# A four-layer graph network on one core: layer 2's early products in batches of six tiles, the totals' maximum ten steps later and pinned, count matrices spread to step 340

## The chip, the cores and the metric

The kernel runs on one core of a Trainium2 chip. A core has five engines that run side by side, each taking its own instructions in order: PE (TensorE, matrix products), DVE (VectorE), ACT (ScalarE), POOL (GpSimd) and SP (SyncE, which here only starts transfers). They meet through semaphores. PE reads SBUF and writes PSUM; DVE and ACT read both. Transfers between HBM and SBUF are started by SP, ACT or POOL. POOL starts the indirect ones (gathers), in which a list in SBUF names a row of a table in HBM for each of 128 partitions.

The metric is device time in microseconds (us). The profile is of one execution. Its matmuls are pipelined and their ends are modelled, so a PE that is busy throughout need not be at its peak.

## The reference

There are N = 6250 nodes with 256 features and E = 100000 edges, sorted by their target `dst`; `src` is random. The targets are dense at small node numbers: up to node n lie about E * sqrt(n / N) edges. The reference applies a layer norm and a relu, and then four graph layers and a last product:

```
deg = segment_sum(1, dst)
h = sage_mean(h):  h @ W1_self + (segment_sum(h[src], dst) / max(deg, 1)) @ W1_neigh + b1
h = sage_pool(h):  hp = relu(h @ W2_pool + b2_pool)
                   h @ W2_self + segment_max(hp[src], dst) @ W2_neigh + b2
h = sage_gcn(h):   ((segment_sum(h[src], dst) + h) / (deg + 1)) @ W3_neigh + b3
h = sage_mean(h):  the form of layer 1, with W4 and b4
return x + h @ W_fc + b_fc
```

Layer 2 is the one that counts here. It takes, for each node, the maximum over the rows `hp[src]` of its incoming edges, and from it and the node's own row the product that layer 3 sums up. The weights of the later layers are multiplied together beforehand, so that layer 2 hands on rows of 512 numbers.

## The kernel before

Nodes are handled in 49 tiles of 128. A row that is summed later is stored split into three bf16 parts (high, middle, low).

**Sums over edges** (layers 1, 3 and 4) are done in two ways. For the first 16 or 18 tiles, whose nodes have many edges, a count matrix says how often each source node occurs for each target node of the tile; the sum is then a dense product of count blocks (fp8, kept in the table `tab_a`) with the split rows. For the other tiles the rows are gathered edge by edge and added with one-hot matrices on PE.

**Layer 2's maximum.** The 100000 edges are laid out in 782 columns of 128 edges, in six blocks of 52, 100, 220, 180, 130 and 100 columns, which are handled from the last block (the largest node numbers) to the first. Each column is one step of the main loop, counted by `at`. In a step POOL gathers 128 rows of `hp` into a buffer X (L1339; a buffer holds two columns and there are six of them), and DVE combines them with the running maximum `run` (L1320, three operations in two steps). SP stores the running maxima that may be needed into `rows2` (L1324). At the end of a block, `carry` passes maxima across the 128 lanes: transposes on PE (L1185, L1208), scans on DVE, a gather (L1200), a maximum (L1211) and a store.

**Beside each step**, the loop issues other work, paced by `at`:

- Count matrices of tiles 8 to 17 (`build_narrow`). Each of 32 columns of a tile takes two one-hots: on DVE a mask `hm` (L363), on ACT `ht` and `hs` (L361, L368). PE multiplies them (L379), ACT copies the counts to the matrix A (L384), and SP stores A to `tab_a` (L388). The 256 columns of tiles 8 to 15 (`first`) are spread evenly from step 16 to step `EARLY_AT` (L1370), the 64 of tiles 16 and 17 (`rest`) from there to step 682 (L1372). One-hots run up to 12 columns ahead.
- `done2(d)`, for each node tile d from 48 down to 0, once the block in which its edges begin is done, and at least 11 steps apart. It is a generator that advances once per step. It gathers the tile's totals from `rows2`, one gather for each block that the tile's edges touch (one or two), and the tile's own rows `th` from `tab_t`. Six steps later it takes the maximum of two totals where there are two (L1235, DVE), and then, a step each: PE transposes (L1239), ACT copies the result to `hTf` (L1242), PE multiplies the own rows with `usA` and `usB` (L1246, L1249) and the maximum with `un` (L1252, two steps), and the sum is split into three bf16 parts `r3` by ACT casts with PE subtractions between (L1260 to L1268). SP stores `r3` to `tab_r`, layer 3's table (L1269).
- Early products of layer 3. As soon as `BATCH` tiles between 6 and 37 have their `r3`, `early_products` queues, for each of the 16 dense tiles of layer 3, a load of the count blocks `ae` (L1296, SP), three matmuls per batch tile (L553) and an addition to the sum `acc3` of that dense tile (L1110, DVE; the first time a copy on ACT, L1113). The loop issues one thirty-second of what is left in each step, at least one piece.

After the last step, the loop at L1400 finishes the tiles still open; tile 0 can begin only there, when the last block is done. Layer 3 gathers from `tab_r`, so its first gather (L472) waits until the last row of the table has landed.

**What sets the order.** The text above is the program's order. The compiler lays out each engine's instructions anew: it takes, by its own estimate of times, the earliest in program order among those that are ready, so work can run before or after its step. `tc.keep_in_program_order(ins)` ties an instruction behind the one that stands before it in the program on the same engine. All buffers of a name come from a ring of `bufs` copies, and an instruction that needs a new one waits until the oldest is free.

Of the kernel before, what the change touches and what calls it, by code (L numbers as in the profile page):

```python
# [9 lines left out]
F32 = mybir.dt.float32  # L10
# [5 lines left out]
ALU = mybir.AluOpType  # L16
# [4 lines left out]
P = 128  # L21
# [10 lines left out]
EARLY = (6, 38)  # L32
MADE_AT = 64
FIRST_AT = 112
EARLY_AT = 250


def _edges_below(n, E, N):
# [40 lines left out]
def fast_path(  # L79
# [15 lines left out]
    nc = tc.nc  # L95
# [10 lines left out]
    KI = FI // P  # L106
    KH = FH // P
# [97 lines left out]
    ident = const.tile([P, P], F32, name="identf")  # L205
# [41 lines left out]
    def bank(pool, tag, name, shape=None, bufs=None):  # L247
        t = pool.tile([P, FH], F32, tag=one_tag.get(id(pool), tag), name=name, **({"bufs": bufs} if bufs else {}))
        if shape is None:
            return t  # L250
        n = math.prod(shape)
        if len(shape) == 1:
            return t[:, :n]
        return t[:, :n].rearrange("p (a b) -> p a b", b=shape[1])
# [387 lines left out]
    with ExitStack() as pro:  # L642
        pst = pro.enter_context(tc.tile_pool(name="pst0", bufs=3, space=PSUM))
        psm = pro.enter_context(tc.tile_pool(name="psm0", bufs=3, space=PSUM))
# [97 lines left out]
        for c in range(NC):  # L742
            nc.tensor.matmul(pc[:, c : c + 1], under[:, c * P : (c + 1) * P], ones_b,
                             start=True, stop=True)
# [208 lines left out]
    with ExitStack() as on:  # L953
        pst = on.enter_context(tc.tile_pool(name="pst1", bufs=1, space=PSUM))
        psm = on.enter_context(tc.tile_pool(name="psm1", bufs=1, space=PSUM))
        psg = on.enter_context(tc.tile_pool(name="psg1", bufs=2, space=PSUM))
        psd = on.enter_context(tc.tile_pool(name="psd1", bufs=2, space=PSUM))
        wk = on.enter_context(tc.tile_pool(name="fl1", bufs=2))
# [4 lines left out]
        def done1(d, acc):  # L963
# [31 lines left out]
            for k in range(KI):  # L995
# [11 lines left out]
                        lambda acc, d=d: todo.append(done1(d, acc)), extra=3)  # L1007
# [107 lines left out]
    with tc.tile_pool(name="fl2c", bufs=1) as ck, ExitStack() as late:  # L1115
# [5 lines left out]
        usA = ck.tile([P, KI, FH], F32, name="usA")  # L1121
        usB = ck.tile([P, KI, FH], F32, name="usB")
# [55 lines left out]
        wk = late.enter_context(tc.tile_pool(name="fl2", bufs=2))  # L1178
# [37 lines left out]
        def totals(d):  # L1216
            tots = []
            for b in range(b_of[d][0], b_of[d][1] + 1):
                t = wk.tile([P, FH], F32, name="tot", bufs=4)
                nc.gpsimd.indirect_dma_start(  # L1220
                    out=t, out_offset=None, in_=rows2[0 : run_at[b] + n_of[b], :],
                    in_offset=bass.IndirectOffsetOnAxis(ap=rows_of[b][:, d : d + 1], axis=0),
                )
                tots.append(t)
            th = wk.tile([P, 2 * KI, P], F32, name="th2", bufs=4)
            nc.scalar.dma_start(th, tab_t[d].rearrange("p (k n) -> p k n", n=P))
            return tots, th

        def done2(d):
            tots, th = totals(d)  # L1230
            for _ in range(6):
                yield
            hm = tots[0]
            for t in tots[1:]:
                nc.vector.tensor_tensor(hm, hm, t, op=ALU.max)  # L1235
            yield
            pt = bank(pst, "pt", "pt_hTf", (KH, P))
            for j in range(KH):
                nc.tensor.transpose(pt[:, j, :], hm[:, j * P : (j + 1) * P], ident)  # L1239
            yield  # L1240
            hT = wk.tile([P, KH, P], F32, name="hTf")
            nc.scalar.copy(hT, pt)  # L1242
            yield
            pm = bank(psm, "pm", "pm_prf")
            for k in range(KI):
                nc.tensor.matmul(pm, th[:, k, :], usA[:, k, :], start=(k == 0), stop=False)  # L1246
            yield
            for k in range(KI):
                nc.tensor.matmul(pm, th[:, KI + k, :], usB[:, k, :], start=False, stop=False)  # L1249
            yield  # L1250
            for c in range(KH):
                nc.tensor.matmul(pm, hT[:, c, :], un[:, c, :], start=False, stop=(c == KH - 1))  # L1252
                if c == 1:
                    yield
            yield
            yield
            yield
            r3 = early_pool[0].tile([P, 3 * FH], BF16, name="r3", bufs=2 * BATCH + 1)
            hi, mid, lo = (r3[:, i * FH : (i + 1) * FH] for i in range(3))
            nc.scalar.copy(hi, pm)  # L1260
            yield
            nc.tensor.matmul(pm, minus_b, hi, start=False, stop=True, skip_group_check=True)
            yield
            nc.scalar.copy(mid, pm)
            yield
            nc.tensor.matmul(pm, minus_b, mid, start=False, stop=True, skip_group_check=True)
            yield
            nc.scalar.copy(lo, pm)  # L1268
            nc.sync.dma_start(tab_r[d * P : (d + 1) * P, :], r3)  # L1269
            if EARLY[0] <= d < EARLY[1]:  # L1270
                ready.append((d, r3))
                if len(ready) == BATCH or d == EARLY[0]:
                    early_products()
            yield


        BATCH = 4
        ready = []
        early = Hub()
        early_pool = []  # L1280
# [6 lines left out]
        def early_products():  # L1287
# [3 lines left out]
            for d in range(H3):  # L1291
                got = {}

                def load(d=d, got=got):
                    got[0] = early_pool[0].tile([P, BATCH, P], F8, name="ae", bufs=LOOK + 3)
                    nc.sync.dma_start(got[0][:, : len(ss), :].bitcast(BF16),  # L1296
                                      tab_a[d, :, ss[0] : ss[-1] + 1, :])
# [29 lines left out]
        tiles, begun2, begun_at = [], 0, 0  # L1327
        ends = []
        now = []
        at = 0  # L1330
        for b in reversed(range(NB)):
# [3 lines left out]
            for s0 in range(0, tb, G2):  # L1335
                X = (xmore if at // G2 % 2 else xpool).tile([P, G2, FH], F32, name="X2")
                for k in range(G2):
                    t = t0 + s0 + k
# [24 lines left out]
                    if at == MADE_AT:  # L1363
                        for _ in steps:
# [3 lines left out]
                            top.enter_context(tc.tile_pool(name="early3", bufs=1)))  # L1368
                    if at <= EARLY_AT:
                        hub.advance(math.ceil(len(first) * max(0, at - 16) / (EARLY_AT - 16)))  # L1370
                    else:
                        hub.advance(len(first) + math.ceil(  # L1372
                            len(rest) * (at - EARLY_AT) / (T - 100 - EARLY_AT)))
                    early.advance(early.done + math.ceil(early.left() / 32))
# [3 lines left out]
                    if (tiles and not ends and at >= begun_at + 11  # L1378
                            and begun2 < NT * (at - FIRST_AT) / (T - 20 - FIRST_AT)):
                        begun_at = at  # L1380
                        now.append(done2(tiles.pop(0)))
                        begun2 += 1
# [9 lines left out]
        tiles += [d for d in reversed(range(NT)) if b_of[d][0] == 0]  # L1392
        while tiles or now:
            if tiles and len(now) < 2:
                now.append(done2(tiles.pop(0)))
            for g in list(now):
                if next(g, 0) == 0:
                    now.remove(g)
# [42 lines left out]
    with ExitStack() as on:  # L1441
        psd = on.enter_context(tc.tile_pool(name="psd3", bufs=2, space=PSUM))
        psg = on.enter_context(tc.tile_pool(name="psg3", bufs=3, space=PSUM))
        psm = on.enter_context(tc.tile_pool(name="psm3", bufs=2, space=PSUM))
# [8 lines left out]
        with tc.tile_pool(name="fl3", bufs=2) as wk:  # L1453
# [36 lines left out]
            for d in range(H3):  # L1490
                work += dense([s for s0, s1 in late for s in range(s0, s1)], lambda s, d=d: block(d, s), lambda s: Z3[s], FH, psd,
                              lambda acc, d=d: todo.append(done3(d, acc)), own=d)
# [3 lines left out]
        with tc.tile_pool(name="fl4", bufs=2) as wk:  # L1496
# [22 lines left out]
            for d in range(H4):  # L1519
                parts4.append(dense([s for s0, s1 in order for s in range(s0, s1)],  # L1520
                                    lambda s, d=d: block(d, s), lambda s: Z4[s], FO, psd,
                                    lambda acc, d=d: todo.append(done4(d, acc)), wide=True))
# [652 lines left out]
```

## Time and profile before

| | |
|---|---|
| median of 3 runs | 2820.56 us (2816.73 to 2822.64) |
| the profiled execution's own time | 2817.91 us |
| its span, first to last instruction | 2816.1 us |
| mean granted PE clock | 0.932 |
| busy over the span: PE, DVE, ACT, POOL | 85%, 74%, 33%, 69% |
| layer 2's gathers L1339, first to last | 784.6 to 1905.4 us |
| layer 3's first gather L472 | 1943.5 us |
| running maxima L1320 on DVE | 758 + 379 operations of 754 and 742 ns, and 24 more |
| masks L363 on DVE | 320 of 280 ns |
| additions L1110 on DVE | 112 of 677 ns |
| early products L553 on PE | 1494 of 1536 recorded |
| totals' gathers L1220 on POOL | 57 of 956 ns |

A row of the page or of the windows gives the busy time of an engine, which is a union of its instructions. What an engine could still take on in a stretch is read from the length of the stretch less that time; what holds it up is read from the waits, which name the instruction or transfer that ended an idle time. POOL's gathers are read by their spacing, since between two of them POOL has about 0.30 us that counts as idle.

### The profile page before, as it was taken

What the parts mean: (1) busy time and instruction counts of PE and PEld (TensorE: products, weight loads), DVE (VectorE), ACT (ScalarE), POOL (GpSimd) and SP (SyncE); (2) the same over time, 40 slices, a digit from 0 to 9 for tenths busy, and PEclk for the clock granted to TensorE, in tenths of its full rate; (3) what the DMA queues carried; (4) which work ended last, traced back from release to release, by engine and by line L of the source; (5) the groups of instructions that cost most, each with busy time, mean ns of one, the idle gap of its engine ahead of it and who ended that gap; (6) DMA issues with size and microseconds to landing.
All of it is one profiled execution on the core that took longest, in us unless ns stands there. A gap on an engine that the chain in (4) does not pass through costs nothing. (4 is left out here: it accounts for less than half of the span.)

```text
span 2816.1 us, 39207 instructions
## 1 busy us (share of the span) xinstructions
PE 2387.7 (85%) x11547; PEld 1280.4 (45%) x11678; DVE 2071.8 (74%) x5431; ACT 934.7 (33%) x2272; POOL 1936.9 (69%) x2257
## 2 busy tenths in 40 slices
PE   3568999999969375797799995985999999999998
PEld 2225666666644132343344442432444444565554
DVE  6976676776479988789889997983566776466665
ACT  3867666665267687521311111100000011000000
POOL 5157777777566676777767777763677776677776
PEclk9669999999999586799899997998999999999999
DMA  5446777777699999999999999996999999788886
GB/s 177 160 135 192 206 208 209 217 220 222 203 317 326 302 348 336 330 361 352 356 317 360 349 353 327 351 305 244 387 379 377 394 371 351 246 241 240 241 241 204
DMA packets 350443, 806.43 MB, mean 286 GB/s; under 512 B 55710, under 2 KB 147334, under 8 KB 350188
## 3 DMA queue, kind: packets, MB, share of 16 engines
q0 software_dynamic: 146160, 514.05, 55.9%
q1 hardware_dynamic: 145976, 234.34, 22.7%
q10 hardware_dynamic: 58084, 55.44, 6.2%
q8 instruction: 94, 1.54, 0.2%
q14 instruction: 129, 1.06, 0.1%
HBM read 605.25 MB, written 199.17 MB: 286 GB/s over the span
## 5 line engine op out<-in xcount | busy, mean ns | idle before, releaser
L1339 POOL DMA_INDIRECT X<-rows,srcIf x782 | 741.7, 949 | 322.4 <-issue 155.0
L1320 DVE SCALAR_TENSOR_TENSOR run<-run,samef,X 128x512 f32<-128x512 f32 x758 | 571.9, 754 | 47.3 <-DMA X<-rows,srcIf 42.3
L494 PE MATMUL pg<-ring,hot 128*128 128x259 bf16 (+1 forms) x2432 | 510.7, 322 | 70.0 <-DMA ring<-tab_h,srcT 47.0
L472 POOL DMA_INDIRECT ring<-tab_h,srcT x474 | 452.2, 954 | 157.7 <-issue 59.1
L523 DVE SCALAR_TENSOR_TENSOR acc<-pg,M,acc 128x256 f32<-128x256 f32 (+2 forms) x694 | 356.6, 539 | 117.7 <-PE pg L494 89.9
L472 POOL DMA_INDIRECT ring<-tab_r,srcE x342 | 332.7, 973 | 130.7 <-issue 57.0
L553 PE MATMUL pd<-r,ae 128*128 128x512 bf16 x1494 | 370.6, 386 | 36.0 <-DVE acc L1110 22.3
L472 POOL DMA_INDIRECT ring<-tab_s,srcE x314 | 299.9, 955 | 114.5 <-issue 33.8
L494 PEld LDWEIGHTS <-hot 128*128 128x128 bf16 x2448 | 240.0, 99 | 294.1 <-issue 134.6
L1320 DVE SCALAR_TENSOR_TENSOR X<-X,samef,run 128x512 f32<-128x512 f32 x379 | 281.4, 742 | 47.3 <-DMA X<-rows,srcIf 17.2
L545 PE MATMUL pd<-zt,ac 128*128 128x512 bf16 x835 | 290.2, 381 | 6.1 <-DMA ac<-tab_a 4.5
L553 PEld LDWEIGHTS <-ae 128*128 128x128 fp8e4 x1536 | 151.9, 99 | 257.4 <-issue 113.1
L546 PE MATMUL pd<-zt,ac 128*128 128x256 bf16 x882 | 241.1, 273 | 2.7 <-DVE zt L305 0.2
L468 DVE TENSOR_SCALAR hot<-iota_bf,keyE 128x128 bf16<-128x128 bf16 x656 | 160.6, 268 | 112.2 <-PE pg L494 80.0
L553 PE MATMUL pd<-zt,ac 128*128 128x512 bf16 x797 | 221.3, 380 | 0.9
L327 ACT ACTIVATE hs<-ht,onef 128x128 bf16<-128x128 bf16 x461 | 173.7, 393 | 85.4 <-PE pb L335 84.0
L1252 PE MATMUL pm_prf<-unf,hTf 128*128 128x512 f32 x392 | 188.4, 606 | 0.5 <-ACT hTf L1242 0.5
L553 PE MATMUL pd<-Z,A 128*128 128x256 bf16 (+1 forms) x1176 | 186.0, 274 | 0.4 <-ACT A L340 0.2
L335 PE MATMUL pb<-hm,hs 128*128 128x392 bf16 x461 | 153.9, 361 | 37.3 <-ACT hs L327 26.5
L468 DVE TENSOR_SCALAR hot<-iota_bf,keyT 128x128 bf16<-128x128 bf16 x474 | 122.1, 266 | 79.1 <-PE pg L494 77.2
L325 ACT ACTIVATE ht<-iota_bf,sk 128x128 bf16<-128x128 bf16 x461 | 171.6, 395 | 20.8 <-DVE sk L836 14.2
L329 DVE TENSOR_SCALAR hm<-iota_w,mk 128x392 bf16<-128x392 f16 x461 | 149.9, 340 | 7.0 <-PE pb L335 6.2
(338 smaller groups left out, 3445.9 us busy)
## 6 DMA issues: line engine op xcount, KB each, us to landing
rows<-X SPq DMA_DIRECT2D x385, 256.0 KB
tab_r<-r SPq DMA_DIRECT2D x49, 384.0 KB
tab_a<-A SPq DMA_DIRECT2D x18, 784.0 KB
tab_t<-th SPq DMA_DIRECT2D x49, 256.0 KB
rows<-hpf SPq DMA_DIRECT2D x49, 256.0 KB
th<-tab_t ACTq DMA_DIRECT2D x49, 256.0 KB
X<-rows,srcIf POOLq DMA_INDIRECT x782, 5.5
ac<-tab_a ACTq DMA_DIRECT2D x90, 112.0 KB
```

Source lines behind the costliest of these rows:

```text
L325: nc.scalar.activation(t, iota_b, AF.Abs, bias=sk[:, r : r + 1])
L327: nc.scalar.activation(hots[0], t, AF.Relu, bias=one, scale=-1.0)
L468: nc.vector.tensor_scalar(hot[j], iota_b, keyT[:, j - jb : j - jb + 1], None, op0=ALU.is_equal)
L472: nc.gpsimd.indirect_dma_start(out=ring[:, j % deep, :], out_offset=None, in_=table, in_offset=bass.IndirectOffsetOnAxis(ap=srcT[:, j - jb ...
L494: nc.tensor.matmul(pg[:, : F + c], hot[j], X[:, part * F : (part + 1) * F + c], start=(k == 0 and part == 2), stop=(k == n - 1 and part == 1),
L523: nc.vector.scalar_tensor_tensor(acc[d], half, m, acc[d], op0=ALU.mult, op1=ALU.add)
L545: nc.tensor.matmul(hold[0], a, z[:, : 2 * F], start=(s == ss[0]), stop=False)
L546: nc.tensor.matmul(hold[0][:, :F], a, z[:, 2 * F :], start=False, stop=(s == ss[-1]))
L553: nc.tensor.matmul(hold[0][:, : F + c], a, z[:, part * F : (part + 1) * F + c], start=(s == ss[0] and part == 2 and s != own), stop=(s == ...
L1252: nc.tensor.matmul(pm, hT[:, c, :], un[:, c, :], start=False, stop=(c == KH - 1))
L1320: nc.vector.scalar_tensor_tensor(put, held, st, row, op0=ALU.mult, op1=ALU.max)
L1339: nc.gpsimd.indirect_dma_start(out=X[:, k, :], out_offset=None, in_=tab_p, in_offset=bass.IndirectOffsetOnAxis(ap=srcI[:, t : t + 1], axis=0),
```

## The change

- Batches of early products have six tiles instead of four (`BATCH`). With it the ring of split rows `r3`, whose size is `2 * BATCH + 1`, grows from 9 to 13 copies, and a load of `ae` covers six blocks. 32 tiles make five batches of six and one of two (tiles 7 and 6), instead of eight of four.
- `hTf` has one copy instead of two.
- In `done2`, tiles with two totals wait ten steps instead of six before the maximum. The maximum (L1235) and the first transpose of every tile (L1239) are tied behind what stands before them on their engine.
- The count matrices of tiles 8 to 15 are spread to step 340 instead of 250 (`EARLY_AT`), and those of tiles 16 and 17 from 340 to 682.
- Tiles begun after the last step (`tail=True`, which is tile 0 alone) issue their own products right after their gathers, ahead of the maximum.

```diff
-EARLY_AT = 250
+EARLY_AT = 340
...
-        def done2(d):
+        def own2(pm, th, w, k0):
+            for k in range(KI):
+                nc.tensor.matmul(pm, th[:, k0 + k, :], w[:, k, :], start=(k0 + k == 0), stop=False)
+
+        def done2(d, tail=False):
             tots, th = totals(d)
-            for _ in range(6):
+            if tail:
+                pm = bank(psm, "pm", "pm_prf")
+                own2(pm, th, usA, 0)
+                own2(pm, th, usB, KI)
+            for _ in range(6 if len(tots) == 1 else 10):
                 yield
             hm = tots[0]
             for t in tots[1:]:
-                nc.vector.tensor_tensor(hm, hm, t, op=ALU.max)
+                tc.keep_in_program_order(nc.vector.tensor_tensor(hm, hm, t, op=ALU.max))
             yield
             pt = bank(pst, "pt", "pt_hTf", (KH, P))
             for j in range(KH):
-                nc.tensor.transpose(pt[:, j, :], hm[:, j * P : (j + 1) * P], ident)
+                turned = nc.tensor.transpose(pt[:, j, :], hm[:, j * P : (j + 1) * P], ident)
+                if j == 0:
+                    tc.keep_in_program_order(turned)
             yield
-            hT = wk.tile([P, KH, P], F32, name="hTf")
+            hT = wk.tile([P, KH, P], F32, name="hTf", bufs=1)
             nc.scalar.copy(hT, pt)
             yield
-            pm = bank(psm, "pm", "pm_prf")
-            for k in range(KI):
-                nc.tensor.matmul(pm, th[:, k, :], usA[:, k, :], start=(k == 0), stop=False)
-            yield
-            for k in range(KI):
-                nc.tensor.matmul(pm, th[:, KI + k, :], usB[:, k, :], start=False, stop=False)
-            yield
+            if not tail:
+                pm = bank(psm, "pm", "pm_prf")
+                own2(pm, th, usA, 0)
+                yield
+                own2(pm, th, usB, KI)
+                yield
...
-        BATCH = 4
+        BATCH = 6
...
             if tiles and len(now) < 2:
-                now.append(done2(tiles.pop(0)))
+                now.append(done2(tiles.pop(0), True))
```

## The prediction

> **What bounds the kernel now.** All edits lie in layer 2, so I first read the windows view, cut where the maximum's gathers (X, L1339) pass steps 60, 120, 260, 340, 420, 460 and 640 of 782.
>
> ```profile
> 784.60:864.30 79.70, 60.69 (x255) 37.77 (x256) 70.05 (x178) 58.80 (x142) 57.69 (x61) 0.92 0.99 351
> 864.30:960.60 96.30, 62.27 (x211) 28.76 (x209) 95.82 (x359) 73.99 (x172) 58.68 (x62) 0.79 0.91 302
> 960.60:1171.40 210.80, 133.10 (x403) 57.18 (x403) 174.64 (x378) 156.52 (x355) 146.93 (x156) 0.75 0.96 341
> 1171.40:1285.30 113.90, 109.35 (x384) 51.25 (x391) 88.60 (x138) 28.10 (x51) 86.18 (x91) 0.98 0.98 345
> ...
> 1389.60:1454.80 65.20, 57.97 (x218) 26.14 (x222) 54.06 (x94) 6.84 (x12) 44.43 (x48) 0.92 0.94 315
> 1454.80:1698.10 243.30, 229.29 (x870) 105.47 (x883) 223.38 (x329) 35.58 (x59) 178.64 (x190) 0.97 1.00 355
> 1698.10:1905.40 207.30, 170.94 (x622) 79.37 (x635) 171.68 (x263) 21.06 (x37) 149.23 (x157) 0.92 0.95 326
> ```
>
> Columns: stretch, length, busy time and count of PE, weight loads, DVE, ACT, POOL, then clock, DMA share, GB/s. Then the page's row of the gathers (busy us, mean ns, idle before):
>
> ```profile
> L1339 POOL DMA_INDIRECT X<-rows,srcIf x782 | 741.7, 949 | 322.4 <-issue 155.0
> ```
>
> and one of them in the timeline (start, us, idle before it):
>
> ```profile
> 1882.72 0.95 POOL L1339 DMA_INDIRECT X<-rows,srcIf  x1 [0.30 <-issue]
> ```
>
> Back to back, an indirect DMA takes POOL 0.95 plus 0.30 us: 1.25 us. Layer 2 issues 782 for X, 55 for totals and 5 for carries before the last X ends: 842 x 1.25 = 1053 us of the 1121 shown. POOL's pace is the floor, and some 67 us above it can be won. By stretch (length minus POOL instructions x 1.25): 3, 20, 17, 0, 2, 6, 7 and 12 us. In the second DVE is full (95.82 of 96.30); from 1455 PE is nearly full.
>
> Next the waits in layer 2 (us in total, times, longest):
>
> ```profile
> DVE tot L1235 <- DMA tot<-rows,rows_of: 35.3, 7, 8.0
> ```
>
> and the timeline behind the longest of them and at the end:
>
> ```profile
> 1881.47 0.94 POOL L1339 DMA_INDIRECT X<-rows,srcIf  x1 [4.13 <-DVE X L1320]
> ...
> 1921.99 0.94 POOL L1220 DMA_INDIRECT tot<-rows,rows_of  x1 [5.94 <-DMA rows<-fixf]
> 1926.67 0.69 DVE L1235 TENSOR_TENSOR tot<-tot 128x512 f32<-128x512 f32 x1 [7.45 <-DMA tot<-rows,rows_of]
> 1928.33 3.12 PE L1246 MATMUL pm_prf<-usA,th 128*128 128x512 f32 x4
> 1931.29 1.88 PE L1249 MATMUL pm_prf<-usB,th 128*128 128x512 f32 x4
> 1933.01 3.60 PE L1252 MATMUL pm_prf<-unf,hTf 128*128 128x512 f32 x8
> 1943.50 0.96 POOL L472 DMA_INDIRECT ring<-tab_r,srcE  x1 [19.31 <-DVE hot L468]
> ```
>
> DVE stands at the totals' maximum while X rows that have landed wait behind it; POOL then runs out of X buffers (the 4.13). After the last gather a serial chain (carry, totals, maximum, transposes, products, casts, store) runs to layer 3's first gather at 1943.50.
>
> **The change part by part.** Base: the profiled execution's 2817.91 us (span 2816.1), 2.65 under the median of 2820.56.
>
> *A. Counts slower up to step 260: -12.* One count column costs DVE a mask (L363, 280 ns), PE, and ACT 0.4 us and more. First matrices: 256 columns in 234 steps (1.09 a step) become 256 in 324 (0.79). The windows of L363 show 52, 67 and 153 masks in the first three stretches. At 0.79 (with the 12 of look-ahead) it would be 94 instead of 119 up to step 120 and 111 instead of 153 after: 67 x 0.28 = 19 us of DVE. Where DVE is full it counts whole (20 masks, 5.6 us), in the first stretch about 1, in the third, where DVE idles 36 of 211 us, half of 11.8. Bounds: 0 (order unchanged) and -19.
>
> *B. The same masks in steps 260 to 340: +2.* 63 masks instead of 16: 47 x 0.28 = 13 us. DVE has 88.6 of 113.9 busy there, so POOL's pace hides them; if that cover is gone, +13. Bounds 0 and +13. PE is at 109 of 113.9; what the counts displace there is early products, in E.
>
> *C. Totals' maximum later and pinned: -10.* Six of the seven waits within the gathers are at two-block tiles 37, 36, 24, 23, 11, 10, the seventh at tile 1. With 10 yields and the pin, a maximum stands at least ten steps (12.5 us) behind its totals' issue; they land in 4.4 to 6.2 us, so the wait goes. Not all 35.3 us were lost: POOL had up to 12 X buffers (15 us) of slack. Its own gaps over 0.30 after these waits are 1.6+2.1+1.2 (1416 to 1437) and 3.8+1.5+1.0+1.4 (1881 to 1903): 12.6. Bounds 0 and -12.6. What is late next is the tile itself: in E.
>
> *D. Six tiles to a batch: -4.* 32 tiles x 16 count tiles x 3 matmuls stay, the bytes too. Sums on DVE fall from 8 x 16 to 6 x 16 (the first 16 are ACT copies): 32 x 0.677 = 21.7 us; loads of ae on SP fall from 128 to 96, each half as long again. From step 340 POOL is the floor, so most of this is off the path: bounds 0 and -15 (27 us over the floor from step 340, less C's 12.6); I take a quarter, since most stretches there sit on the floor. SP waits at ae loads for PE 50 times, at most 4.0 us, with X's stores behind; half longer is 6, below the 15 us of slack: nothing, and past 15 a microsecond each. One hTf buffer: the pin puts the next transposes behind the products that read it, so nothing; without that, one ACT copy's wait per tile.
>
> *E. Early products later: +5.* In the saturated windows 1540 to 1680, 400 loads (133 triples) and 7 tiles fill 140 us: 0.64 us a triple and 7.7 us a tile (16 f32 passes at 0.43 plus transposes and subtractions). The transposes, now pinned behind the PE instruction traced before, can no longer run ahead: in the trace tile 37 turned at step 253 though the loop begins it at 273. By the loop's rules batches are complete at steps 347, 423, 505, 583, 703, 725 (before: 325, 370, 423, 483, 529, 583, 681, 725; the trace began the seventh 14 steps early, at 667). If tile 8 ends the fifth batch at 697: 128 triples (82 us) and tiles 6 to 2 (5 x 7.7) are 120 us, against 85 X and 8 other gathers, 116 us, plus 6 us until the last X is through: PE just ends in time. Tile 1's maximum now comes behind the carry's, in PE's idle time. At 703 with tile 7 also open: 128 - 105 - 6 = 17 late. I take +5; bounds 0 and +40 (rival 1).
>
> *F. Own products first in the last tile: -3.* Its eight own passes (1928.33 to 1932.6) move ahead of the totals' landing; the other product starts when hTf is there (1929.22) instead of 1932.6: 3.4. If PE is slow after idling (first group 3.12 against 1.88), 2.1. Bounds 0 and -3.4.
>
> Sum: -12+2-10-4+5-3 = -22: 2796; plus 2.65, **2798**.
>
> Against B and the first half of A speaks a rule of the Trainium skill (SBUF — State Buffer, "Who interferes with whom"): a tensor_scalar in a two-port mode locks GpSimd out of the port through which it writes descriptors. By it the 47 masks moved to where POOL is the floor would cost 13 us there, and the total would be 2809. The trace disagrees: with two one-hots per gather in layer 1 an indirect DMA takes 954 ns and 56 go in 70 us, as here without masks (949, 56).
>
> **The rivals.**
> 1. *PE ends late (slower).* Place: tiles 13 to 8, after the third carry. PE must fit 128 triples of early products into the gathers left. If pinned tiles run one after another and the batch waits until step 725, and a triple takes the 0.73 us of the slowest row (six early products in 1.46 us at 1894.12), 93 + 4 x 7.7 = 124 us stand against 62 x 1.25 + 6 = 84: 40 us late, straight onto the carry's transposes at 1912. 2798 - 5 + 40 = 2833. Past 28 us it eats the whole gain, and the run is measurably slower past 33, a start past step 715. For it: PE 229 of 243 us in the seventh stretch. Against: PE idles 36 us of the last, and begun tiles allow step 703.
> 2. *Floor reached.* All bounds: -19+0-12.6-15+0-3.4 = -50: 2771. For it: POOL stalls mostly name DVE as the releaser. Against: the carry's waits (2.4, 1.8) and a stall of 8.2 at 1069.6, where SP waits for a count matrix, are untouched.
> 3. *The spread does nothing.* The compiler's order moves work forward when an engine seems free (33 of the 64 late masks ran by step 280), so freed slots may fill again: A and B 0, sum -12: 2809.
> 4. *Masks block POOL.* Each of B's 47 masks holds up POOL's issue for its 280 ns, where POOL is the floor: B is +13, 2798 + 11 = 2809. Against: 954 ns per indirect DMA beside two one-hots in layer 1, 949 here. (This is the rule named above.)
>
> **How the numbers follow.** My forecast 0.46 (own range 2783 to 2813), rival 1 0.24, rival 2 0.13, rival 3 0.12, rival 4 0.05. A measurement of this kernel tells about 0.2%, 5.6 us. Faster: 0.43 of the forecast, 0.13, 0.07 and 0.03: 0.66. Same: 0.02, 0.04 of rival 1, 0.04, 0.02: 0.12. Slower: the rest, 0.22, nearly all rival 1. Range 2768 (rival 2 and a little) to 2834 (rival 1).
>
> **What would show it.** A: the masks' windows 94 and 111, DVE below full before 960. C: no wait at the maximum within the gathers, tile 37's transposes near step 283. D: 80 sums of L1110's kind. E: the first early matmul 50 steps later, the fifth batch's near 697, no PE work between the last X and the carry's transposes. F: the last tile's second product starts with its hTf. Wrong if the time from first to last X does not fall by 20 us, or the time from last X to layer 3's first gather (38 us) grows.

## The result: slower by 0.7%, and the profile after

The changed kernel takes 2843.82 us (median, 2835.84 to 2847.95) against 2822.48 us for the kernel before in the same comparison: a ratio of 1.0071, estimated over all five executions of each (the two medians alone would give 1.0076), with a 95% interval of 1.0056 to 1.0086. All ratios below are of this kind. The forecast was 2798 us, with a range of 2768 to 2834. The sign was wrong and the time lies outside the range. The profiled execution after took 2843.82 us (span 2842.0).

The difference of the two spans, 25.9 us, splits at three points of POOL's gathers (start of the first X, end of the last X, layer 3's first gather):

| | before | after | |
|---|---|---|---|
| up to the first X | 784.6 | 787.3 | +2.7 |
| first X to the end of the last X | 1120.8 | 1111.8 | -9.0 |
| end of the last X to layer 3's first gather ("the end") | 38.1 | 67.5 | +29.4 |
| layers 3 and 4 | 872.6 | 875.5 | +2.9 |

So the gathers became shorter, by less than forecast, and the end became 29.4 us longer. First the windows view of the changed kernel, cut where its gathers (now L1348) pass the same steps 60, 120, 260 and so on, and one window over its end (columns as in the prediction):

```profile
787.30:868.80 81.50, 61.45 (x259) 38.20 (x259) 69.51 (x171) 59.57 (x144) 57.60 (x62) 0.92 0.98 346
868.80:959.70 90.90, 56.02 (x174) 26.13 (x175) 88.90 (x331) 48.29 (x111) 59.02 (x61) 0.80 0.93 314
959.70:1164.20 204.50, 127.78 (x382) 55.17 (x381) 172.16 (x360) 134.34 (x306) 148.19 (x157) 0.76 0.97 345
1164.20:1276.80 112.60, 81.31 (x265) 35.90 (x266) 97.62 (x200) 69.11 (x155) 84.17 (x89) 0.82 0.98 351
...
1443.00:1689.20 246.20, 230.23 (x872) 105.50 (x870) 213.72 (x315) 42.04 (x75) 182.52 (x192) 0.99 0.99 353
1689.20:1899.10 209.90, 169.70 (x637) 76.45 (x636) 169.54 (x260) 18.65 (x33) 146.60 (x155) 0.93 0.94 319
1905.00:1945.00 40.00, 38.63 (x148) 18.14 (x148) 14.95 (x29) 4.59 (x8) 2.84 (x3) 1.00 0.24 73
```

Read two lines of it. In the fourth (steps 260 to 340) PE's busy time has fallen to 81.31 of 112.60 us, where it was 109.35 of 113.90 before: PE idles there now. In the last one, after the gathers, PE is busy for 38.63 of 40 us; in the same window before it was 21.00:

```profile
1905.00:1945.00 40.00, 21.00 (x60) 9.61 (x59) 12.22 (x35) 6.34 (x11) 4.41 (x6) 0.82 0.37 123
```

Work has moved from a place where PE had time to the place where everything waits for it. Before, PE had no early product left to do when the last X was through; now 101 recorded matmuls of L553 (38 us) come after it.

The row of the gathers and the waits at the totals' maximum (now L1243) show that POOL's pace is as it was and that most of the waits are gone:

```profile
L1348 POOL DMA_INDIRECT X<-rows,srcIf x782 | 743.4, 951 | 318.3 <-issue 140.5
```

```profile
DVE tot L1243 <- DMA tot<-rows,rows_of: 12.9, 2, 6.8
```

Of these 12.9 us, 6.8 belong to the last tile, after the gathers (7.45 before). Within the gathers one wait of 6.0 us is left, at 1748 us, of seven (35.3 us) before. The forecast had none left. The carry of block 2 came to its maximum at 1735.5 us (1701.6 before), so the totals of that tile were gathered only from 1741.6 on, too late for its place in DVE's list.

The timeline of the end shows what took their place:

```profile
1938.97 1.46 PE L553 MATMUL pd<-r,ae 128*128 128x512 bf16 x6
...
1940.48 0.60 PE L1185 MATMUL ptcf<-identf,X 128*128 128x128 f32 x4
...
1943.75 0.69 DVE L1211 TENSOR_TENSOR fixf<-fixf,pcf 128x512 f32<-128x512 f32 x1 [0.45 <-PE pcf L1208]
...
1947.23 0.94 POOL L1220 DMA_INDIRECT tot<-rows,rows_of  x1 [36.03 <-PE pt_hTf L1247]
...
1951.87 0.69 DVE L1243 TENSOR_TENSOR tot<-tot 128x512 f32<-128x512 f32 x1 [6.83 <-DMA tot<-rows,rows_of]
```

DVE finishes the last block's running maxima at 1906.4 us. The transposes of the last carry (L1185) read these maxima. They start at 1940.48, 34 us later, and PE comes to them without an idle time: its list has early products (L553) and the tiles 3 and 2 ahead of them. Before, the same transposes started 0.7 us behind the last maximum, which ended at 1911.45:

```profile
1912.19 0.60 PE L1185 MATMUL ptcf<-identf,X 128*128 128x128 f32 x4
```

Everything that follows is late by what PE is late: the carry's maximum, the last totals (POOL has stood idle for 36 us before them), their maximum and layer 3's first gather at 1966.6. From the transposes to that gather it now takes 26.1 us, against 31.3 before, so the end has grown by less than PE's 34 us.

The other carries tell the same. From the gather to the maximum of the carries of blocks 5 to 0 it took 16.4, 15.6, 8.4, 4.8, 20.5 and 3.4 us before, and 19.9, 9.4, 14.3, 48.2, 64.9 and 33.5 us after.

### The profile page after: what moved, and what is told of

Its sections match the earlier page's. It is cut to its first block, busy times and chain, and to the rows that moved or that the text cites. A ratio compares the mean times of both kernels' runs of the same rounds, so it can differ in the third digit from the quotient of the medians.

```text
span 2842.0 us, 39243 instructions
## 1 busy us (share of the span) xinstructions
PE 2401.3 (84%) x11678; PEld 1277.9 (45%) x11678; DVE 2058.0 (72%) x5399; ACT 933.0 (33%) x2272; POOL 1938.0 (68%) x2257
## 4 chain that ended last, share of the span: by engine, by line
PE 42%; DMA 33%; DVE 12%; issue 6%; POOL 6%; ACT 1%; ACTq 0%; SPq 0%; POOLq 0%; DVEq 0%
DMA X<-rows,srcIf 13%; PE pg L494 10%; PE pd L553 9%; DMA ring<-tab_h,srcT 5%; DMA ring<-tab_s,srcE 4%; DVE run L1329 4%; PE pd L545 4%; POOL X L1348 3%; DMA rows<-X 3%; PE pm_hp L993 3%; DVE X L1329 3%; PE pm_hp L996 3%; DMA ring<-tab_r,srcE 3%; PE pm_w L269 2%; PE pd L546 2%
## 5 line engine op out<-in xcount | busy, mean ns | idle before, releaser
L1348 POOL DMA_INDIRECT X<-rows,srcIf x782 | 743.4, 951 | 318.3 <-issue 140.5
L553 PE MATMUL pd<-r,ae 128*128 128x512 bf16 x1536 | 371.8, 386 | 37.7 <-DVE acc L1110 35.3
L545 PE MATMUL pd<-zt,ac 128*128 128x512 bf16 x882 | 306.4, 382 | 6.6 <-DMA ac<-tab_a 5.1
L553 PEld LDWEIGHTS <-ae 128*128 128x128 fp8e4 x1536 | 152.2, 99 | 266.7 <-issue 115.4
L553 PE MATMUL pd<-zt,ac 128*128 128x512 bf16 x816 | 224.3, 379 | 0.0
L553 PE MATMUL pd<-Z,A 128*128 128x256 bf16 (+1 forms) x1176 | 186.4, 274 | 0.6 <-ACT A L340 0.4
L1261 PE MATMUL pm_prf<-unf,hTf 128*128 128x512 f32 x392 | 180.7, 593 | 0.1
L325 ACT ACTIVATE ht<-iota_bf,sk 128x128 bf16<-128x128 bf16 x461 | 171.5, 395 | 21.0 <-DVE sk L836 14.3
L379 PE MATMUL pb<-hm,hs 128*128 128x196 bf16 x320 | 68.2, 277 | 109.0 <-DVE hm L363 89.6
```

The source lines that it names most:

```text
L325: nc.scalar.activation(t, iota_b, AF.Abs, bias=sk[:, r : r + 1])
L545: nc.tensor.matmul(hold[0], a, z[:, : 2 * F], start=(s == ss[0]), stop=False)
L553: nc.tensor.matmul(hold[0][:, : F + c], a, z[:, part * F : (part + 1) * F + c], start=(s == ss[0] and part == 2 and s != own), stop=(s == ...
L1348: nc.gpsimd.indirect_dma_start(out=X[:, k, :], out_offset=None, in_=tab_p, in_offset=bass.IndirectOffsetOnAxis(ap=srcI[:, t : t + 1], axis=0),
```

## The experiments

Four theories of why PE is late: the pins hold the tiles back (1); a batch of six stands ahead of the carries (2); the slower counts push PE's work back (3); the end is long by its own order and not by the amount of work (4). The first four runs are the changed kernel with one thing undone. They ran on another chip than all others, one on which the kernel before takes 3369.0 us (median), so their ratios, all to the kernel before on that chip, say only which way each part pulls. Gathers and ends are those of the one profiled execution of each run. Between nearly equal kernels the gathers of such single executions differ by up to 10 us (1109.0 for the spread alone, 1118.6 with the last tile's edit beside it), so a few us there settle nothing by themselves.

**Early products of the last two batches left out.** Edit to the changed kernel, in `early_products`:

```diff
             ready.clear()
+            if ss[0] < 14:
+                return
```

> The changed kernel with the early products of tiles 13 to 6 left out altogether (the last two batches, 128 triples, 82 us of PE; these products are missing from the result). Theories 1 and 2 (PE's work ends late, whatever made it late): the carry's transposes after the last X come at once, the end falls from 67.5 to 36 us or less, total about 2805 to 2815. Theory 4 (the end is long because of its own order, tile 1's maximum pinned behind the carry's): the end stays at 60 us or more, total 2835 or more.

Measured: 0.9932 (0.9897 to 0.9968), the end 33.8 us, and the last carry's transposes (2292.3 us) directly behind the last maximum (2292.2). So the end is long because of the early products that PE still has ahead of it, and not by its own order of instructions. Since the run does less work, its ratio prices nothing.

**Counts spread to step 250 again, batches of four again, no pins.**

```diff
-EARLY_AT = 340
+EARLY_AT = 250
```

> The changed kernel with the count matrices spread to step 250 again. The changed kernel takes 29 us longer than the one before from the last X gather to layer 3's first gather (67.5 instead of 38.1), and 9 us less from the first X gather to the last. Theory 1 (the pins hold back the tiles, PE idles near step 270 and its work ends late): the pins are still here, so the end stays near 65 us; the X gathers take about as long as before or a little more (1112 to 1125); total 2840 to 2852. Theory 2 (batches of six stand in front of the carries' transposes on PE): the same, 2840 to 2852. Theory 3 (the slower counts push PE's work back): the end falls to about 40 us and the total to about 2822.

```diff
-            hT = wk.tile([P, KH, P], F32, name="hTf", bufs=1)
+            hT = wk.tile([P, KH, P], F32, name="hTf")
...
-        BATCH = 6
+        BATCH = 4
```

> The changed kernel with batches of four tiles (a ring of nine split rows and two hTf buffers) again. Theory 1 (pins): the end stays 55 us or longer, PE still idles some 30 of the 40 us near step 270, total 2835 or more. Theory 2 (batches of six in front of the carries' transposes): the carry of block 2 takes from gather to maximum some 5 us instead of 48, the end falls to about 40 us, total about 2815 to 2820. Theory 3 (slower counts): as in theory 1.

```diff
-            for _ in range(6 if len(tots) == 1 else 10):
+            for _ in range(6):
...
-                tc.keep_in_program_order(nc.vector.tensor_tensor(hm, hm, t, op=ALU.max))
+                nc.vector.tensor_tensor(hm, hm, t, op=ALU.max)
...
-                if j == 0:
-                    tc.keep_in_program_order(turned)
```

> The changed kernel without the two pins and with six steps before every maximum; batches of six, spread to 340 and the last tile's own products stay. Theory 1 (pins): PE is busy again between 1160 and 1200 us, early products start about 30 us sooner, the end falls to about 40 us; with the gain in the X gathers kept the total is 2800 to 2818. Theory 2 (batches of six): the end stays above 55 us, total 2835 or more. Theory 3 (slower counts): as theory 2.

Measured: 1.0056 (1.0013 to 1.0099) with an end of 71.4 us; 0.9998 (0.9974 to 1.0022) with 52.2; 0.9994 (0.9964 to 1.0024) with 49.2. Taking back the spread does not shorten the end, which speaks against theory 3; with four-tile batches or without pins it is shorter, and neither alone brings it back to 38: both ends lie between what the theories said. These intervals are too wide to settle shares between theories 1 and 2. So the next four runs took each part by itself, on a chip where the kernel before takes 2827.85 us. The later runs were on two further chips, where it takes 2827.81 and 2827.57.

**The changed kernel again, beside its parts.** No edit.

> The changed kernel itself, unchanged, so that its ratio stands beside those of its parts on one chip. All theories: 1.005 to 1.009 of the kernel before; time from the last X gather to layer 3's first gather (the end) 60 to 75 us. If it is within 0.2% of the kernel before, the loss depends on the chip, and the first chip's price of the end (29 us) isn't to be explained by the code alone.

Measured: 1.0072 (1.0045 to 1.0099), end 66.4 us. The loss is there again.

**The spread alone** (the kernel before with `EARLY_AT = 340`).

> The kernel before with one edit: count matrices spread to step 340 (A and B alone; the early products then start later by the loop's rules too). Theory 3 (slower counts alone push the products of layer 3 to the end): end over 50 us against 38 before, ratio 1.000 to 1.006. Theories 1 (pinned maximum and transposes hold the tiles back) and 2 (batches of six stand ahead of the carries' transposes): end 36 to 45 us, time from first to last X shorter by 5 to 12 us, ratio 0.996 to 0.999.

Measured: 0.9973 (0.9957 to 0.9989), gathers 1109.0 us (11.8 less), end 39.1. This part gains, and theory 3 falls.

**The pins alone** (the kernel before with the ten steps, the pinned maximum and the pinned transposes).

> The kernel before with one edit: the totals' maximum ten steps behind the loads and pinned, the transposes pinned (C alone; counts as before, batches of four). Theory 1 (the pins hold tiles back, PE idles early and is late at the end): end over 50 us, PE idle at least 15 us more around step 270, ratio 1.001 to 1.008. Theories 2 and 3: the waits at the maximum within the gathers gone (29 us less), end 36 to 45, ratio 0.996 to 0.999.

Measured: 1.0028 (1.0015 to 1.0041). The gathers take 1112.5 us, 8.3 less, but the end is 51.9 us, 13.8 more; the last carry's transposes start 15 us behind the last maximum (1919.4 against 1904.2).

**Batches of six alone.**

```diff
-            hT = wk.tile([P, KH, P], F32, name="hTf")
+            hT = wk.tile([P, KH, P], F32, name="hTf", bufs=1)
...
-        BATCH = 4
+        BATCH = 6
```

> The kernel before with one edit: six tiles to a batch and one hTf buffer (D alone; counts and maximum as before). Theory 2 (batches of six): the sums fall from 112 to 80, but batches are complete later, end over 50 us, gather to maximum of the carries of blocks 2 and 1 over 30 us (4.8 and 20.5 before), ratio 1.001 to 1.008. Theories 1 and 3: end 36 to 45, ratio 0.997 to 1.000.

Measured: 1.0052 (1.0036 to 1.0069), gathers 1123.3 us (2.5 more), end 57.3 (19.2 more), the carries of blocks 2 and 1 28.8 and 43.0 us, the first just under the 30 expected. Theories 1 and 2 both hold, each for a part of the loss. Two questions stayed: which of the pins, and what about a batch of six.

**Batches of six, issued more slowly.** The loop issues a share of the early products that are left in each step. A full batch of four is 64 triples, so 1/32 of it is two triples a step; a full batch of six is 96, so three. Three triples at the prediction's 0.64 us are 1.9 us of PE in a step of 1.25 us. The edit to the kernel before with batches of six:

```diff
-                    early.advance(early.done + math.ceil(early.left() / 32))
+                    early.advance(early.done + math.ceil(early.left() / 48))
```

> The kernel before with batches of six and one hTf buffer, and the share of the waiting early products that one step issues lowered from 1/32 to 1/48 (a full batch of six then begins with two triples a step, as a batch of four does, not three). Theory burst (three triples a step are 3 x 0.64 = 1.9 us of PE where a step has 1.25, so tiles and carries fall behind): gather to maximum of the carries of blocks 2 and 1 under 25 us (28.8 and 43.0 with 1/32), last batch's first add before X 750 (770), end 38 to 46, ratio 0.998 to 1.002. Theory late (the batch is complete later, and what is left then doesn't fit): the last batch starts where it did, end 55 or more, ratio 1.004 or more.

Measured: 0.9994 (0.9983 to 1.0006), end 40.4 us, the carries of blocks 2 and 1 23.1 and 21.2 us. The carry of block 1, gather and maximum, in the timelines of the kernel before, of batches of six, and of batches of six issued more slowly:

```profile
1841.39 0.94 POOL L1200 DMA_INDIRECT fixf<-rows,fixIf  x1 [0.30 <-DMA rows<-X]
...
1861.93 0.68 DVE L1211 TENSOR_TENSOR fixf<-fixf,pcf 128x512 f32<-128x512 f32 x1
```

```profile
1847.47 0.94 POOL L1200 DMA_INDIRECT fixf<-rows,fixIf  x1 [0.30 <-issue]
...
1890.51 0.68 DVE L1211 TENSOR_TENSOR fixf<-fixf,pcf 128x512 f32<-128x512 f32 x1
```

```profile
1850.39 0.95 POOL L1200 DMA_INDIRECT fixf<-rows,fixIf  x1 [0.30 <-issue]
...
1871.55 0.68 DVE L1211 TENSOR_TENSOR fixf<-fixf,pcf 128x512 f32<-128x512 f32 x1
```

20.5, 43.0 and 21.2 us. One miss stands against the expectation: the last batch's first addition came at X 768, not before 750. The last batch is as late as before, and the early products run on to 1934 us as they did in batches of six. But now the carry's transposes start at 1921.6, 0.8 us behind the last maximum, and 49 recorded early matmuls run beside and behind the serial end. The cost of a batch of six is the place of its products in PE's list, ahead of the carries, and not their amount.

**The transposes' pin alone** (the kernel before with this one pin).

> The kernel before with the transposes' pin alone (maximum where it was, counts and batches as before). Theory transposes (the pin on PE keeps a tile's transposes from running ahead): first early product near 1248 as with both pins, against 1208 before, end 45 to 55, ratio 1.002 to 1.006. Theory maximum (the later, pinned maximum does it): first early product within 15 us of 1208, end 36 to 42, ratio 0.999 to 1.001.

Measured: 0.9990 (0.9977 to 1.0003), end 40.9, first early product at 1218.1 us, 10 us later than before. This pin does no measurable harm: the maximum must do it. The next four kernels (two on this chip, two on the next) are a two by two of the maximum's two edits, on top of the spread and the new last tile, with batches of four and without the transposes' pin.

**Spread and last tile alone, and with both edits of the maximum.**

> The kernel before with the counts spread to step 340 and the last tile's own products first (A, B and F; batches of four, no pins, six steps). Beside the spread alone (0.9973, end 39.1): F at its forecast gives end 34 to 37 and 0.996; if the own products stand in the way of the carry's transposes, end 40 or more and 0.9975 or more. Either way faster than both kernels.

> As the kernel with spread and tail, and the totals' maximum ten steps behind its loads and pinned, but without the transposes' pin. Theory transposes: the waits at the maximum within the gathers go (29 us less) and PE is not late: end 33 to 40, first to last X 1097 to 1107, ratio 0.990 to 0.995, the best of all. Theory maximum: end over 45, ratio 0.999 or more.

**Ten steps without the pin, the pin with six steps.**

> The kernel with spread and tail (0.995, end 36.8, tile 37's maximum at step 253 or so), with ten steps before a two-block tile's maximum and no pin. Theory pin (the compiler's order brings an unpinned maximum forward whatever the steps, so only the pin makes the tile late): tile 37's maximum before step 262, first early product before 1220 us, end 34 to 40, ratio 0.993 to 0.997. Theory steps (four steps more are what makes the tiles late): first early product at 1225 or later, end over 42, ratio 0.997 or more.

> The kernel with spread and tail, with the totals' maximum pinned and the six steps kept. Theory pin: tile 37's maximum at step 272 or later, first early product at 1225 us or later, end over 42, ratio 0.997 or more. Theory steps: end 34 to 40, ratio 0.993 to 0.997. By either, waits at the maximum within the gathers under 15 us in all, since the pin leaves at least six steps (7.5 us) after its loads' issue, which land in 4.4 to 6.2.

In the table the step is counted by DVE's running maxima, three to two steps, and the waits include some 7 us of the last tile, after the gathers.

| steps before the maximum | pinned | ratio to before | end, us | tile 37's maximum at step | waits at the maximum, us |
|---|---|---|---|---|---|
| six | no | 0.9950 (0.9932 to 0.9967) | 36.8 | 251 | 36.0 |
| ten | no | 0.9948 (0.9925 to 0.9971) | 34.5 | 255 | 34.4 |
| six | yes | 0.9970 (0.9956 to 0.9985) | 45.1 | 275 | 7.4 |
| ten | yes | 0.9975 (0.9961 to 0.9989) | 46.8 | 279 | 6.7 |

The forecast that the kernel with spread and tail beats both was met; that with both edits of the maximum is at 0.9975 where the theory of the maximum said 0.999 or more, its end as that theory has it. The pin costs some 0.2% and eight to twelve microseconds at the end; the four steps do nothing that shows. The reason for the longer end is in the order that the compiler lays out. It brings an unpinned maximum forward by about 20 steps, and with it the tile's transposes and products, into a time in which PE idles. Tile 37's maximum with the transposes that wait for it, and the first early product, in the timeline with ten steps and no pin:

```profile
1171.92 0.68 DVE L1243 TENSOR_TENSOR tot<-tot 128x512 f32<-128x512 f32 x1
1172.65 1.11 PE L1247 MATMUL pt_hTf<-identf,tot 128*128 128x128 f32 x4 [1.57 <-DVE tot L1243]
...
1214.66 2.75 PE L553 MATMUL pd<-r,ae 128*128 128x512 bf16 x12
```

and in that with ten steps and the pin:

```profile
1202.10 0.68 DVE L1243 TENSOR_TENSOR tot<-tot 128x512 f32<-128x512 f32 x1
1202.84 1.11 PE L1247 MATMUL pt_hTf<-identf,tot 128*128 128x128 f32 x4 [1.13 <-DVE tot L1243]
...
1239.06 2.75 PE L553 MATMUL pd<-r,ae 128*128 128x512 bf16 x11
```

30 us later for the maximum, 24 for the first early product. With the pin the other two-block tile's maximum even comes first, at 1181.18 (PE's first transposes wait for the second maximum, so I take that for tile 37's and the first for tile 36's). The pin took 28 us of waits from DVE, but the gathers became only 9.5 and 10.9 us shorter, since most of the waits were covered by POOL's loaded buffers; the end became 12.3 and 8.3 us longer. So within the single profiled executions gain and loss in layer 2 nearly cancel. The net 0.2% is in the executions' times (2811.5 against 2818.6 us on one chip, 2813.9 against 2819.2 on the other, as means of 7 and 12), and the profiles do not show in which stretch it is lost.

**The change, mended.** The changed kernel with six unpinned steps and 1/48; batches of six, spread, last tile and transposes' pin stay.

```diff
-            for _ in range(6 if len(tots) == 1 else 10):
+            for _ in range(6):
...
-                tc.keep_in_program_order(nc.vector.tensor_tensor(hm, hm, t, op=ALU.max))
+                nc.vector.tensor_tensor(hm, hm, t, op=ALU.max)
...
-                    early.advance(early.done + math.ceil(early.left() / 32))
+                    early.advance(early.done + math.ceil(early.left() / 48))
```

> The changed kernel with its two costly edits mended: the totals' maximum after six steps and not pinned, and 1/48 of the waiting early products issued in a step in place of 1/32; spread, tail, batches of six and the transposes' pin stay. If the parts add up (0.9950 x 0.9994 x 0.9990): 0.993 to 0.995, end 36 to 42, so 13 to 15 us under the kernel before and 33 us under the changed one. If pin and batches of six get in each other's way: end over 45, ratio 0.998 or more.

Measured: 0.9977 (0.9961 to 0.9993), end 41.8 us, carries of blocks 2 and 1 25.7 and 27.9 us. It beats both kernels, but by less than the product of its parts, and lies between the two forecasts. The kernel with spread and last tile alone is the simplest that does better: 2814.27 us, 0.9950 of the kernel before, so about 1.2% under the changed one (0.9950 / 1.0072). That with ten unpinned steps (2813.26 us) can't be told from it.

**The parts together.** Spread with last tile 0.9950, pins 1.0028, batches of six 1.0052: the product is 1.0030, and the change measures 1.0072. Each factor is uncertain by some 0.0015, so the product by some 0.003; that the two losses add up to more than their sum is likely, and not more. The trace shows one place where they meet. The carry of block 2 takes 4.8 us before, 22.6 with the pins alone, 28.8 with batches of six alone and 48.2 with both, and the next tiles' totals are gathered only behind it. No run isolates the joint part.

## Why the prediction was wrong

**The steps that failed are D's price and E's size.** D took batches of six as a matter of sums on DVE and loads on SP, bounded it between 0 and -15 us and took -4. Alone it cost 0.52%, +14.7 us of 2828. The rule that one step issues a thirty-second of what is left stood in the description of the loop, and the prediction did not apply it to the larger batch: three triples a step in place of two. With 1/48 the part is worth -1.7 us (bounds -4.8 to +1.7), which fits D's own argument that the saved sums lie off the path.

E asked whether PE's last work fits, which was the right question, and answered it with terms that were too small. Its sum was 128 triples (82 us) and five tiles (38.5), 120 us from step 697 on. In the changed kernel the fifth batch's first early matmul is at 1798.38 (its first addition at X 712), and the carry's transposes start at 1940.48. PE's rows in this stretch (window 1799.0 to 1940.5 us, the costliest):

```profile
L553 PE MATMUL pd<-r,ae 128*128 128x512 bf16 x355 | 89.6, 388 | 8.9 <-DVE acc L1110 8.3 <-DMA tab_r<-r 0.6
L1261 PE MATMUL pm_prf<-unf,hTf 128*128 128x512 f32 x44 | 20.7, 592 | 0.0
L551 PE MATMUL pd<-r,ident_b 128*128 128x512 bf16 x24 | 9.8, 407 | 4.6 <-DVE acc L1110 4.6
L1231 PE MATMUL pm_prf<-usA,th 128*128 128x512 f32 x20 | 9.4, 592 | 0.0
L1231 PE MATMUL pm_prf<-usB,th 128*128 128x512 f32 x20 | 9.4, 592 | 0.0
```

Columns: busy us and mean ns, then idle us before them. From 1798.4 to the carry's transposes PE needs 142 us, 128 of them busy, and the last maximum is there after 108. What E lacked: the start at 712 (15 steps, some 19 us), the 24 matmuls with the identity that give a dense tile its own rows (L551, 9.8 us and named nowhere in the prediction), and 13 us in which PE waits for DVE to empty a sum's bank (L1110). The late start is itself a matter of the late carry of block 2. But the start alone does not explain the end: batches of six alone begin their fifth batch at X 698, next to E's 697, and their last carry's transposes are still 12 us late (1936.0 against 1924.2). E's bounds, 0 to +40, held the measured +29.4; the value taken, +5, did not.

**C's gain was in part luck, and its price was looked for in the wrong place.** The waits at the maximum within the gathers fell from 35.3 us to 6.0, and the pins alone shortened the gathers by 8.3 us, near the forecast 10. But 7.1 of the 8.3 lie ahead of step 260, where no two-block tile takes its maximum. Past step 340, where C had its 12.6 us, POOL is 23.7 us over its pace with the pins alone and 26.3 before. These profiles do not bear out where C saw the waits cost time. And the tiles then come late: the net is +7.9 us. The prediction blamed the pinned transposes for what E might cost. The pin of the transposes alone is 0.9990; it is the maximum's pin. Having seen that the trace begins work up to 20 steps before the loop, the prediction should have asked what a pinned DVE instruction does to the PE work behind it.

**A and B were right, F only in its first half.** The stretches up to step 260 lie 29 us over POOL's pace (length less POOL's instructions x 1.25) against 40 before, -11 for the forecast -12, though the masks ran otherwise than forecast: 87 up to step 120 (94) and 132 after (111). Thirteen profiles of the faster chips agree: 28 to 36 us over it (31 on average) with the spread to 340, 35 to 48 (42) with that to 250. DVE is still full between steps 60 and 120 (88.90 of 90.90 us). Steps 260 to 340 lie 1.4 us over the pace with 76 masks, where the forecast was +2. The spread alone measured -0.27%, 7.6 us, against -10 for A and B.

F's second product does start with its hTf, in the kernel with spread and last tile at 1929.08 us. But PE has been idle for 7.5 us before the tile's transposes, and the eight matmuls now take 6.43 us, where they took 3.60:

```profile
1929.08 6.43 PE L1259 MATMUL pm_prf<-unf,hTf 128*128 128x512 f32 x8 [0.73 <-ACT hTf L1250]
```

The loss of a first group after idling, which F saw in the own products (3.12 against 1.88), has moved to the product that F left behind them. From the last totals' maximum to layer 3's first gather it takes 16.0 us, against 16.9 with the spread alone: 0.9 for the forecast 3. In the kernel with ten unpinned steps tile 1's product keeps PE busy up to the last tile's transposes, and the same way takes 13.1 us.

**The rivals.** Rival 1 is what happened, at its place and by its mechanism, and 34 us late where it said 40; only its condition, a start at step 725, was not needed. It had 0.24, and its price of 2833 kept the -24 us that A to D were to save in the gathers; these gave -9.0: from step 340 on, where C and D were to save 14 us, POOL is 30 us over its pace (26 before), perhaps since late carries hold back the totals there; no run takes that apart, and one kernel without either loss (spread and last tile) shows 31 in its profile too. Its turning point (a start past step 715) was meant to decide the sign, and the sign turned at 712, with batches of six alone even at 698: the threshold rested on the same short sum as E. Rival 2 needed the gains of C and D. Rival 3 falls with the spread's 0.9973. Rival 4 falls with steps 260 to 340: 89 POOL instructions in 112.6 us, 1.27 us each, with 76 masks beside them, and an indirect DMA of X still takes 951 ns. The 179 gathers of X that a mask overlaps by 0.2 us or more take 947 ns on average, the 548 that none overlaps 950. The rule of the Trainium skill (SBUF — State Buffer, "Who interferes with whom"), that DVE's two-port modes keep GpSimd from its descriptors, does not show in this kernel's masks; whether they run in such a mode no row tells.

The test named for the whole, that the gathers must shorten by 20 us and the end not grow, marked the failure at once: 9.0 and +29.4.

## What to carry to other kernels

When an engine is nearly full in the last stretch, list every instruction that it must do between the latest start and the first thing that the end waits for, by rows, and compare the sum with the time; a start that slips is paid in full there, or more (here 14 steps, from X 698 with batches of six alone to 712, and 22 us, from 12 to 34 us late). A pace that is a share of what is left changes when the pieces grow, so a batch size and its divisor belong together. An order that is pinned to spare one engine a wait also pins the work of the engines behind it: ask first whether the wait was covered, and then where the work behind it will stand.

## What the hardware showed beside this

One chip ran the kernel before at 3369 us, 19% slower than the 2828 us of another. In the four profiles taken there POOL's spacing was the same (a median of 1251 to 1254 ns), and the gathers as long (950 to 953 ns). Much of what was longer is idle time for which the profile shows no cause. The waits of the changed kernel with batches of four on that chip, and then of the same kernel less the transposes' pin on one of the others (us in total, times, longest):

```profile
PEld L553 <- issue: 290.2, 471, 19.4
POOL ring L472 <- issue: 241.1, 773, 0.9
POOL X L1348 <- issue: 223.1, 631, 2.2
```

```profile
POOL ring L472 <- issue: 141.3, 450, 0.7
POOL X L1346 <- issue: 140.2, 458, 1.0
PEld L553 <- issue: 105.0, 267, 7.1
```

The transfers ran at 241 GB/s over the span there and at 286 here, and the mean granted clock of PE was 0.891 against 0.929. What slows that chip stays open; for a comparison it means that both kernels have to run on the same one.
